# The queries' maxima spread over the partitions: three bfloat16 rows in place of a float32 product with diagonal tiles

## The chip, the cores and the metric

The kernel runs on one core of a Trainium2 chip. The metric is the device time of one execution in microseconds (us). Runs of the same kernel are compared by their median.

## What is computed

The input x has 4 batches of 2048 tokens of 512 features, in float32. Two layers follow each other. The first is causal attention with one head of width 512 and with relu on its projections; the second is a feed-forward layer with two top-32 gates. The change lies in the attention:

```python
q = jax.nn.relu(x @ Wq + bq)
k = jax.nn.relu(x @ Wk + bk)
v = jax.nn.relu(x @ Wv + bv)
e = jnp.einsum('bqd,bkd->bqk', q, k) / jnp.sqrt(jnp.float32(D))
...
e = e - NEG * causal[None, :, :]
e = jnp.exp(e - jnp.max(e, axis=-1, keepdims=True))
attn = e / jnp.sum(e, axis=-1, keepdims=True)
y = jnp.einsum('bqk,bkd->bqd', attn, v)
return jax.nn.relu(y @ Wo + bo)
```

What matters here is the maximum of each query's scores, which is subtracted before the exponential.

## The kernel before

The tokens are worked on in 16 groups of 512 (four groups g = 0 to 3 in each batch), each of four tiles of 128 tokens. Phase 1 (`phase1`) does the attention, the residual sum and the norms; phase 2 (`phase2`) does the feed-forward layer tile by tile. Between them the results go through memory. A second branch of the program, with `every_key=True`, is there for inputs with very large scores; it holds the same functions and is not executed here.

Scores are kept with keys on the partitions: a score tile `n.st[kt]` has 128 keys on the partitions and the group's 512 queries along the free dimension. So the maximum over the keys is a maximum across partitions, and it has to be available on every partition, along the free dimension, to be subtracted. This is how it is made:

- VectorE folds the score tiles into `n.mx` (128 x 512) with elementwise maxima (`masked` L688, `maximum` L589).
- `fold` (L707) turns its four 128x128 blocks on TensorE into PSUM (L711).
- `reduced` (L714) takes the maximum along the free dimension on VectorE (L717). The result is 128 x 4: query q of tile t stands in partition q, column t.
- `diagonals` (L720) multiplies the identity by each of the four columns on VectorE (L725). This gives four 128x128 tiles with the maxima on their diagonals.
- `spread` (L727) multiplies a 128x128 tile of ones with these 512 columns in one float32 product on TensorE (L730). Every partition of `n.mb` in PSUM then holds all 512 maxima.
- `weights` (L732) subtracts `n.mb` from each score tile on VectorE (L738), takes the exponential on ScalarE (L739) and sums up on GpSimd (L743).
- `attend` (L768) multiplies the weights with the values (L773), and `summed` (L748) takes the sums over the keys.

The matrix products are float32, and the profile shows each as two matmul instructions (two passes). Projections and products with keys of earlier groups are done by class `Seven` (L523) with seven block products in place of eight; each of its steps `p1` to `p7` is eight matmul instructions of 256 columns (L555). A step that ends an accumulation is written out by `written` (L592): VectorE adds a partial result (L607) and ScalarE applies bias and relu (L614).

The order of the work is written out by hand in `steps` (L906) for TensorE, VectorE and GpSimd. ScalarE's order is left to the framework's scheduler; some of its instructions have a raised priority (`tc.high_priority()`). TensorE's order is the program's. VectorE's order comes from a small planner, `Pace` (L224): it keeps a modelled time of TensorE (`pace.pe(us)` moves it on) and of VectorE, and it puts queued jobs (`pace.add(rank, job)`) into VectorE's stream where the model says that there is time; `pace.flush(job)` puts a job there at once if it is not there yet. Around the change (L976 to L989) the order is: `fold`; the job `diagonals` is queued at rank 0; then the steps Q.p2, Q.p5, V.p7, Q.p1 and V.p4 of the next group's projections; then `spread` and the queuing of `weights`. In the last group there is no next group: two pieces of a filler, `bound` (L861, matmuls L869, followed by an activation L877 on ScalarE), stand between `fold` and `spread`.

In phase 2, `logits` (L1215) begins with a bfloat16 product of three rows (L1218): `ones3`, a 3 x 128 tile of ones, with a bias that is stored as three bfloat16 rows whose sum is the float32 bias. A product of one column (L1428) stands near the end of phase 2.

Of the kernel before, what the change touches and what calls it, by code (L numbers as in the profile page):

```python
# [28 lines left out]
F32 = mybir.dt.float32  # L29
BF16 = mybir.dt.bfloat16  # L30
I32 = mybir.dt.int32
AF = mybir.ActivationFunctionType
ALU = mybir.AluOpType
# [6 lines left out]
P = 128  # L40
GT = 512
TPG = GT // P
# [11 lines left out]
def sandwich_kernel(ctx: ExitStack, tc: tile.TileContext, io: dict, out: bass.AP):  # L54
    nc = tc.nc
    x = io["L0_attn_x"]
    B, S, D = x.shape
    C2 = io["L0_ffn_weight"].shape[1]
    NG = io["L0_ffn_so_conv_w"].shape[0]
    NC = D // P  # L60
# [10 lines left out]
    const = ctx.enter_context(tc.tile_pool(name="const", bufs=1))  # L71
    dram = ctx.enter_context(tc.tile_pool(name="dram", bufs=1, space=DRAM))

    ident = const.tile([P, P], F32, name="ident")
    make_identity(nc, ident)

    causal = const.tile([P, P], F32, name="causal")
    nc.gpsimd.memset(causal, 0.0)
# [3 lines left out]
    ones = const.tile([P, P], F32, name="ones")  # L82
# [30 lines left out]
    ones3 = const.tile([3, P], BF16, name="ones3")  # L113
# [82 lines left out]
    def phase1(every_key):  # L196
# [8 lines left out]
        sm = enter("sm", 4)  # L205
        two = enter("two", 2)
# [8 lines left out]
        ps_tp = enter("ps_tp", 2, space=PSUM)  # L215
# [4 lines left out]
        def combine(out, a, b, op, factor=1.0):  # L220

            nc.vector.scalar_tensor_tensor(out, a, factor, b, ALU.mult, op)  # L222
# [54 lines left out]
        pace = Pace()  # L277

        def work(us, fn, *args, pause=0.0):

            fn(*args)
            yield us, pause
# [34 lines left out]
        def at_once(pieces):  # L317
            for _ in pieces:
                pass
# [81 lines left out]
        parts = lambda m: [(AS_RIGHT if m == "o" else AS_LEFT)[k] for k in ORDER]  # L401
# [305 lines left out]
        def fold(src):  # L707

            tp = ps_tp.tile([P, NC, P], F32, name="tp")
            for t in range(TPG):  # L710
                nc.tensor.transpose(tp[:, t, :], src[:, t * P : (t + 1) * P], ident)  # L711
            return tp

        def reduced(tp, op):  # L714

            r = sm.tile([P, TPG], F32, name="fold")
            nc.vector.tensor_reduce(r, tp, axis=AX.X, op=op)  # L717
            return r

        def diagonals(n, tp):  # L720

            m = reduced(tp, ALU.max)
            n.dg = two.tile([P, TPG, P], F32, name="xn")
            for t in range(TPG):
                nc.vector.tensor_scalar_mul(n.dg[:, t, :], ident, m[:, t : t + 1])  # L725

        def spread(n):  # L727

            n.mb = ps_mm.tile([P, GT], F32, name="mm")
            nc.tensor.matmul(n.mb, lhsT=ones, rhs=n.dg.rearrange("p t q -> p (t q)"), start=True, stop=True)  # L730

        def weights(n):  # L732

# [127 lines left out]
        def bound():  # L861

            w = ring.take("q", range(NC))
            for d in range(NC):
                ps = ps_mm.tile([P, GT], F32, name="mm")
                for c in range(NC):
                    nc.tensor.matmul(  # L869
                        ps, lhsT=w[c][1][:, d * P : (d + 1) * P], rhs=w[c][1], start=(c == 0), stop=(c == NC - 1)  # L870
                    )
                    if c % 2:
                        pace.pe(1.72)
                    if c == 1:
                        yield
                sqr = prp.tile([P, D], F32, name="pr")
                nc.scalar.activation(sqr, ps, AF.Square, accum_out=squared[:, 0, d : d + 1])  # L877
                yield

        def prepare(br):  # L880

            j = branches.index(br)
            nc.sync.dma_start(gamma2[:, j : j + 1], io[f"L0_ffn_{br}_gamma"].rearrange("(p o) -> p o", o=1))
            nc.sync.dma_start(beta2[:, j : j + 1], io[f"L0_ffn_{br}_beta"].rearrange("(p o) -> p o", o=1))
            lin, left = (stp.tile([P, D], F32, name="st") for _ in range(2))
            nc.sync.dma_start(
                lin.rearrange("p (c g) -> p c g", c=NC), io[f"L0_ffn_{br}_lin_w"].rearrange("(c p) g -> p c g", p=P)
            )
            nc.sync.dma_start(left[0:1, :], io[f"L0_ffn_{br}_lin_b"].rearrange("(o n) -> o n", o=1))
            return lin, left[0:1, :]  # L890

        def bias_rows(br, left):

            wide = prp.tile([P, D], F32, name="pr")[0:1, :]
            for k in range(3):
                row = prep.tile([1, C2], BF16, name="row")
                nc.vector.tensor_copy(row, left)
                nc.sync.dma_start(lin_3[br][k : k + 1, :], row)
                if k < 2:
                    nc.vector.tensor_copy(wide, row)  # L900
                    combine(left, left, wide, ALU.subtract)
                yield 1.5, 2.0
# [3 lines left out]
        def steps(n, ahead):  # L906
# [3 lines left out]
            for j in range(NGRP):  # L910
                nxt = ahead
                last = nxt is None
                filler = bound() if last else None
                if j in (1, 2):
                    lin, left = prepare(branches[j - 1])
# [43 lines left out]
                else:  # L959
                    V = Seven(nxt, "v")  # L960
# [15 lines left out]
                if ahead is not None:  # L976
                    measured = pace.add(1, moments(ahead), 2.0)
                tp = fold(n.mx)
                dg = pace.add(0, work(1.8, diagonals, n, tp))
                pace.pe(0.45)  # L980
                if last:
                    next(filler), next(filler)
                else:
                    Q = Seven(nxt, "q")
                    Q.p2(), Q.p5(), V.p7(), Q.p1(), V.p4()
                pace.flush(dg)
                spread(n)
                pace.pe(0.86)
                weighted = pace.add(1, weights(n))  # L989
                if not last:  # L990
                    if stored:
# [14 lines left out]
                if j in (1, 2):  # L1006
                    br = branches[j - 1]
                    transposed(ps_tp, lin, lin_T[br].rearrange("p (c o) -> p c o", c=NC), nc.scalar.copy)
                    rows = pace.add(1, bias_rows(br, left))
                if last:  # L1010
                    next(filler)

# [23 lines left out]
                            behind.append(pace.add(2, chain(n, u), 2.0))  # L1036
                pace.flush(*evicted)
                if j in (1, 2):
                    pace.flush(rows)
                if last:  # L1040
                    pace.drain()
                    features(n, 0)
# [9 lines left out]
                before, n = n, nxt  # L1052
# [4 lines left out]
        n = load(*order[0], queues=(nc.sync, nc.sync if every_key else nc.scalar))  # L1057
# [15 lines left out]
        if every_key:  # L1073
            bo = broadcast(wp, "L0_attn_bo")
            for b in range(B):
                kTs, vos = [], []
                for g in range(GB):
                    if b + g:
                        n = load(b, g)
                        at_once(moments(n))  # L1080
                    transpose_x(n)
                    drop(project(n, "v"))
                    drop(project(n, "k"))
                    drop(project_vo(n))
                    kTs.append(n.kT)
                    vos.append(n.vo)
                for g in range(GB):
                    n = load(b, g)
                    at_once(moments(n))
                    transpose_x(n)  # L1090
                    drop(project(n, "q"))
                    no_scores(n)
                    for kt in range(n.nk):
                        score_tile(n, kt, kTs[kt // TPG])
                    diagonals(n, fold(n.mx))
                    spread(n)
                    at_once(weights(n))
                    inverses(n, summed(n.sum))
                    n.a, n.xg, n.xr = [None] * TPG, [None] * TPG, [None] * TPG
                    for t in range(TPG):  # L1100
                        load_residual(n, t)
                        attended(n, t, attend(n, t, vos))
                        at_once(chain(n, t))
                        if n.i == NGRP - 1:
                            features(n, t)
                    if n.i < NGRP - 1:
                        fetch_features(n.i)
                        pace.drain()
        else:

            transpose_x(n)
            ahead = load(*order[1])
            at_once(moments(ahead))
            for m in "vqk":
                w = project(n, m)
                weight_sums(m, w)
                if m == "k":
                    squares(w)
                drop(w)
            w = project_vo(n)  # L1120
            ahead.ahead = [normed(ahead, t) for t in range(2)]
            weight_sums("o", w)
            drop(w)
            head.close()

            bo = broadcast(wp, "L0_attn_bo")
            for br in branches:
                nc.gpsimd.dma_start(
                    conv_w[br],
                    io[f"L0_ffn_{br}_conv_w"].rearrange("g f -> (g f)").rearrange("(o n) -> o n", o=1).broadcast_to((P, D)),  # L1130
                )
            with tc.manual_schedule(engines={PE, mybir.EngineType.DVE, mybir.EngineType.Pool}):
                steps(n, ahead)
# [346 lines left out]
```

## Time and profile before

| | |
|---|---|
| median of 3 runs | 2429.8 us (2428.56 to 2430.73) |
| the profiled execution | 2428.93 us |
| its span in the trace | 2427.1 us |
| granted TensorE clock, mean | 0.994 |
| TensorE matmul busy | 2374.7 us (98%) |
| VectorE busy | 1796.1 us (74%) |
| ScalarE busy | 1118.2 us (46%) |
| L730, product with the diagonals | 32 matmul instructions in 16 groups, 592 ns each |
| L725, diagonals | 64 instructions, 281 ns each |
| L717, maximum along the free dimension | 16 instructions, 680 ns each |
| L1218, product of three bfloat16 rows | 128 matmul instructions, 374 to 384 ns each |

The span is the time from the first to the last instruction in the trace; the execution's own time is 1.8 us longer. Lines of the profile name the engine (PE is TensorE, DVE VectorE, ACT ScalarE, POOL GpSimd), the line of the kernel, the operation, the tile written and the tiles read, the shape, and the count. Matmuls overlap: a matmul's duration is longer than the time until the next one starts, so the time that a row of matmuls takes from TensorE is read from the starts. In lines of the timeline the first column is the start in us from the span's start, the second the duration, and what stands in brackets at the end is the idle time of the engine before it and what ended it.

### The profile page before, as it was taken

To read this page: it belongs to the slowest core of one execution; us is meant where nothing else is said; L and a number is where in the kernel's file an instruction comes from. 1 tells how busy PE (TensorE), PEld (TensorE's weight loads), DVE (VectorE), ACT (ScalarE), POOL (GpSimd) and SP (SyncE) were. 2 spreads that over 40 slices of the span, in tenths; PEclk is the share of its full clock that TensorE was granted. 3 is DMA by queue.
4 is the path that set the end of the run, shared out by engine and by line. 5 is a ranking of instruction groups with operands and counts; after the bars stand their busy time and mean duration, and the time that the engine had idled before them with its cause. 6 is when DMAs were issued, how large, how long until landed. Compare 5 with 4: busy or idle time off the path is not lost.

```text
span 2427.1 us, 29394 instructions
## 1 busy us (share of the span) xinstructions
PE 2374.7 (98%) x8418; PEld 1531.5 (63%) x8418; DVE 1796.1 (74%) x3941; ACT 1118.2 (46%) x2352; POOL 900.7 (37%) x856
## 2 busy tenths in 40 slices
PE   8999999999999999999999999999889999999997
PEld 3776858587685858768585776857334444444443
DVE  3587775558866555886655588655599999999998
ACT  2333423233342323334233334322268888888887
POOL 1012211311221031122103112211269999999997
PEclk9999999999999999999999999999999999999999
DMA  6587755568775656876565677633433444444441
GB/s 222 179 244 203 215 166 166 145 178 236 217 204 165 165 144 183 227 220 202 168 166 142 184 224 211 194 117 88 121 74 98 112 122 113 122 113 118 117 122 54
DMA packets 594735, 392.18 MB, mean 162 GB/s; under 512 B 393090, under 2 KB 460162, under 8 KB 594564
## 3 DMA queue, kind: packets, MB, share of 16 engines
q1 hardware_dynamic: 590932, 386.53, 57.6%
q10 hardware_dynamic: 3312, 2.63, 0.4%
q8 instruction: 70, 1.15, 0.2%
q0 software_dynamic: 320, 1.05, 0.1%
q14 instruction: 101, 0.83, 0.1%
HBM read 275.26 MB, written 114.82 MB: 161 GB/s over the span
## 4 chain that ended last, share of the span: by engine, by line
PE 73%; DVE 19%; ACT 3%; issue 3%; POOL 1%; DMA 0%; POOLq 0%; ACTq 0%
PE acc L555 24%; PE acc L773 19%; PE mm L555 17%; PE mm L673 5%; DVE m_si L1227 4%; DVE rest_so L1235 3%; DVE m_so L1227 3%; DVE rest_si L1235 3%; PE mm L1294 2%; PE mm L408 2%; DVE rest_so L1238 2%; DVE rest_si L1238 1%; ACT sq L1268 1%; PE lg L1220 1%; ACT sq L1265 1%
## 5 line engine op out<-in xcount | busy, mean ns | idle before, releaser
L773 PE MATMUL acc<-vo,st 128*128 128x512 f32 x1088 | 475.9, 593 | 0.0
L773 PEld LDWEIGHTS acc<-vo,st 128*128 128x128 f32 x1088 | 205.3, 190 | 239.8 <-issue 234.3
L1294 PE MATMUL mm<-w_L_ffn_weight,xsT 128*128 128x512 f32 x512 | 232.0, 596 | 2.6 <-ACT xsT L165 1.4
L1294 PE MATMUL mm<-w_L_ffn_weight,xnT 128*128 128x512 f32 x512 | 232.1, 596 | 0.0
L137 POOL TENSOR_TENSOR rs_a<-ve_a,neg_half 128x1 f32<-128x1 f32 x64 | 38.4, 600 | 489.7 <-DVE ve_a L146 483.7
L1294 PEld LDWEIGHTS mm<-w_L_ffn_weight,xsT 128*128 128x128 f32 x512 | 98.0, 192 | 127.0 <-issue 113.4
L1294 PEld LDWEIGHTS mm<-w_L_ffn_weight,xnT 128*128 128x128 f32 x512 | 97.7, 191 | 122.1 <-issue 118.2
L555 PE MATMUL mm<-xnT,wb 128*128 128x256 f32 x720 | 170.1, 379 | 0.0
L555 PE MATMUL acc<-T,wb 128*128 128x256 f32 x720 | 170.1, 379 | 0.0
L743 POOL TENSOR_TENSOR mxsum<-mxsum,st 128x512 f32<-128x512 f32 (+2 forms) x144 | 162.5, 1128 | 14.7 <-ACT st L739 4.3
L137 POOL TENSOR_TENSOR rstd_x<-var_x,neg_half 128x4 f32<-128x4 f32 (+1 forms) x19 | 17.8, 936 | 403.1 <-DVE var_x L310 398.8
L555 PE MATMUL acc<-xnT,wb 128*128 128x256 f32 x720 | 165.2, 379 | 0.0
L555 PEld LDWEIGHTS acc<-xnT,wb 128*128 128x128 f32 x720 | 136.8, 190 | 25.0 <-issue 6.5
L555 PEld LDWEIGHTS acc<-T,wb 128*128 128x128 f32 x720 | 136.8, 190 | 25.0 <-issue 6.5
L555 PEld LDWEIGHTS mm<-xnT,wb 128*128 128x128 f32 x720 | 135.3, 190 | 24.0 <-issue 7.2
L673 PE MATMUL mm<-qT,kT 128*128 128x128 f32 (+3 forms) x512 | 148.6, 433 | 0.0
L574 ACT COPY cp<-mm 128x512 f32<-128x512 f32 x72 | 42.2, 586 | 203.6 <-PE mm L555 200.0
L222 DVE SCALAR_TENSOR_TENSOR mxsum<-mxsum,st 128x512 f32<-128x512 f32 (+2 forms) x144 | 86.4, 600 | 65.9 <-ACT st L601 61.3
L1227 DVE MAX8 m_si<-rest_si 128x8 f32<-128x512 f32 x192 | 130.4, 679 | 0.1
L1227 DVE MAX8 m_so<-rest_so 128x8 f32<-128x512 f32 x192 | 128.9, 671 | 0.0
L1235 DVE MATCH_REPLACE8 rest_so<-m_so,rest_so 128x512 f32<-128x512 f32 x192 | 128.8, 671 | 0.0
L1235 DVE MATCH_REPLACE8 rest_si<-m_si,rest_si 128x512 f32<-128x512 f32 x192 | 128.8, 671 | 0.0
(238 smaller groups left out, 4902.1 us busy)
## 6 DMA issues: line engine op xcount, KB each, us to landing
wb<-keys SPq DMA_DIRECT2D x168, 256.0 KB, 2.9
x<-x SPq DMA_DIRECT2D x124, 256.0 KB, 3.0
xr<-in_L_attn_x_dram SPq DMA_DIRECT2D x64, 256.0 KB, 3.8
xn<-xn SPq DMA_DIRECT2D x64, 256.0 KB, 2.8
out_dram<-h SPq DMA_DIRECT2D x64, 256.0 KB, 2.0
xt<-in_L_attn_x_dram SPq DMA_DIRECT2D x62, 256.0 KB, 3.2
wb<-Z_v SPq DMA_DIRECT2D x60, 256.0 KB, 2.8
wb<-Z_q SPq DMA_DIRECT2D x60, 256.0 KB, 3.1
```

The lines of the kernel that those rows point to most:

```text
L137: nc.gpsimd.tensor_tensor(dst, src, neg_half[:, : src.shape[1]], ALU.pow)
L222: nc.vector.scalar_tensor_tensor(out, a, factor, b, ALU.mult, op)
L408: nc.tensor.matmul(ps, lhsT=w[c][1][:, d * P : (d + 1) * P], rhs=xnT[:, c, :], start=(c == 0), stop=(c == NC - 1))
L555: nc.tensor.matmul(ps[:, d * H : (d + 1) * H], lhsT=left[:, c, d * P : (d + 1) * P], rhs=right[:, c, :], start=(new and c + d == 0), stop= ...
L574: nc.scalar.copy(t, ps)
L673: nc.tensor.matmul(ps[:, off:], lhsT=kT[:, c, k : k + P], rhs=n.qT[:, c, off:], start=(c == 0), stop=(c == NC - 1),)
L743: nc.gpsimd.tensor_tensor(n.sum[:, off:], n.sum[:, off:], w, ALU.add)
L773: nc.tensor.matmul(acc, lhsT=n.st[kt][:, t * P : (t + 1) * P], rhs=vos[kt // TPG][:, kt % TPG, :], start=(kt == 0), stop=(kt == nk - 1),)
L1227: nc.vector.max(n.m8[br], n.rest[br] if k else n.lg[br])
L1235: nc.vector.match_replace(n.rest[br], n.m8[br], n.rest[br], -LOWEST)
L1238: nc.vector.match_replace(n.rest[br], n.m8[br], n.lg[br], -LOWEST)
L1294: nc.tensor.matmul(ps, lhsT=lhsT[:, c, :], rhs=wf[:, c, :], start=(c == 0), stop=(c == NC - 1))
```

## The change

The step `diagonals` is replaced by two, `thirds` on VectorE and `rows` on TensorE and ScalarE, and `spread` is made from what these give.

- `thirds` splits the 128 x 4 maxima into three bfloat16 parts whose sum is the float32 value: it copies to bfloat16, copies back to float32, subtracts, and so on. These are seven small VectorE instructions, each of which reads the result of the one before.
- `rows` turns the parts, tile by tile, with a bfloat16 identity: four matmuls, each with three stationary columns and 128 moving columns, give a 3 x 512 tile in PSUM. ScalarE copies it to SBUF as bfloat16.
- `spread` multiplies `ones3` (three rows) with these 512 columns in one bfloat16 product.
- In the order of the work, `rows` goes ahead of V.p4, and `spread` stays behind V.p4. In the last group, `rows` goes between the two filler pieces. The planner's figures change with it: 1.3 in place of 1.8 us for the VectorE job, and 0.25 at `rows` and 0.25 at `spread` in place of 0.86 us of TensorE.
- A bfloat16 identity is made once at the start. A variable is renamed from `rows` to `linear`.

```diff
+    ident16 = const.tile([P, P], BF16, name="ident16")
+    nc.vector.tensor_copy(ident16, ident)
...
-        def diagonals(n, tp):
+        def thirds(n, tp):
 
             m = reduced(tp, ALU.max)
-            n.dg = two.tile([P, TPG, P], F32, name="xn")
+            n.parts = sm.tile([P, 3, TPG], BF16, name="parts")
+            wide = sm.tile([P, TPG], F32, name="wide")
+            for k in range(3):
+                nc.vector.tensor_copy(n.parts[:, k, :], m)
+                if k < 2:
+                    nc.vector.tensor_copy(wide, n.parts[:, k, :])
+                    combine(m, m, wide, ALU.subtract)
+
+        def rows(n):
+
+            tp = ps_tp.tile([P, NC, P], F32, name="tp")
             for t in range(TPG):
-                nc.vector.tensor_scalar_mul(n.dg[:, t, :], ident, m[:, t : t + 1])
+                nc.tensor.matmul(
+                    tp[0:3, t, :],
+                    lhsT=n.parts[:, :, t],
+                    rhs=ident16,
+                    start=(t == 0),
+                    stop=(t == TPG - 1),
+                    skip_group_check=True,
+                )
+            n.rows = two.tile([P, 2 * D], BF16, name="xn")[0:3, :GT]
+            with tc.high_priority():
+                nc.scalar.copy(n.rows, tp[0:3, :, :].rearrange("p t q -> p (t q)"))
+            pace.pe(0.25)
 
         def spread(n):
 
             n.mb = ps_mm.tile([P, GT], F32, name="mm")
-            nc.tensor.matmul(n.mb, lhsT=ones, rhs=n.dg.rearrange("p t q -> p (t q)"), start=True, stop=True)
+            nc.tensor.matmul(n.mb, lhsT=ones3, rhs=n.rows, start=True, stop=True)
...
                 tp = fold(n.mx)
-                dg = pace.add(0, work(1.8, diagonals, n, tp))
+                dg = pace.add(0, work(1.3, thirds, n, tp))
                 pace.pe(0.45)
                 if last:
-                    next(filler), next(filler)
+                    next(filler)
+                    pace.flush(dg)
+                    rows(n)
+                    next(filler)
                 else:
                     Q = Seven(nxt, "q")
-                    Q.p2(), Q.p5(), V.p7(), Q.p1(), V.p4()
-                pace.flush(dg)
+                    Q.p2(), Q.p5(), V.p7(), Q.p1()
+                    pace.flush(dg)
+                    rows(n)
+                    V.p4()
                 spread(n)
-                pace.pe(0.86)
+                pace.pe(0.25)
                 weighted = pace.add(1, weights(n))
...
-                    diagonals(n, fold(n.mx))
+                    thirds(n, fold(n.mx))
+                    rows(n)
                     spread(n)
```

More of the change, by code (lines that the diff above doesn't have):

```diff
@@ L1008, in steps @@
                     transposed(ps_tp, lin, lin_T[br].rearrange("p (c o) -> p c o", c=NC), nc.scalar.copy)
-                    rows = pace.add(1, bias_rows(br, left))
+                    linear = pace.add(1, bias_rows(br, left))
                 if last:
@@ L1038, in steps @@
                 if j in (1, 2):
-                    pace.flush(rows)
+                    pace.flush(linear)
                 if last:
```

## The prediction

> **What bounds the kernel now.** I read the page's busy shares first, then who waited for whom on TensorE in the first phase, then the timeline of TensorE around one group's product L730, then ScalarE and VectorE in the same microseconds, and last the places where the kernel already runs what the change brings in: a bfloat16 product of three rows (L1218) and a stationary tile with very few columns (L1428).
>
> ```profile
> PE 2374.7 (98%) x8418; PEld 1531.5 (63%) x8418; DVE 1796.1 (74%) x3941; ACT 1118.2 (46%) x2352; POOL 900.7 (37%) x856
> ```
>
> That is an average over two phases. The first phase, where the change lies, is read from a window and from TensorE's waits in it:
>
> ```profile
> 20.00:1742.00 1722.00, 1720.66 (x6696) 1244.00 (x6696) 1123.91 (x2286) 564.07 (x1112) 304.52 (x328) 1.00 0.64 181
> ```
>
> ```profile
> PE acc L555 <- DVE vo L607: 1.3, 4, 0.4
> ```
>
> In 1722 us TensorE is idle for 1.3, at full clock; VectorE works 1124, ScalarE 564. So the first phase lasts as long as its stream of matmuls, and the sum for this change is one of TensorE time, plus any wait that it puts into the stream. What it saves on VectorE is worth nothing by itself. The stream around the product that goes, in the first group:
>
> ```profile
> 96.41 1.89 PE L555 MATMUL acc<-T,wb 128*128 128x256 f32 x8
> 98.13 1.02 PE L730 MATMUL mm<-xn,ones 128*128 128x512 f32 x2
> 98.99 1.89 PE L555 MATMUL mm<-xnT,wb 128*128 128x256 f32 x8
> ```
>
> Starts count here, since the ends are modelled and overlap. L730 holds the stream from 98.13 to 98.99: 0.86 us, two passes of 0.43. There is one per group, 16 in all. The block of 96.41 is V.p4, ahead of which the new transposes go.
>
> **What the change removes.** 16 x 0.86 = 13.8 us of TensorE, and on VectorE four multiplications per group (L725, 281 ns each, one begun every 0.2 us, 0.87 together).
>
> **What it adds on TensorE.** Two visits per group from the float32 stream to bfloat16 products that use a part of the array: four 128x128 transposes onto three columns, and one product of three rows with 512 columns. The second exists already, in the second phase:
>
> ```profile
> 1795.12 0.60 PE L164 MATMUL tp<-ident,xs 128*128 128x128 f32 x4
> 1795.65 0.39 PE L1218 MATMUL lg<-lin_si,ones 3*128 3x512 bf16 x1
> 1795.88 0.37 PE L1218 MATMUL lg<-lin_so,ones 3*128 3x512 bf16 x1
> 1796.18 1.12 PE L1220 MATMUL lg<-linT_si,xa_si 128*128 128x512 f32 x2
> 1797.14 1.02 PE L1220 MATMUL lg<-linT_so,xa_so 128*128 128x512 f32 x2
> 1798.00 0.59 PE L1294 MATMUL mm<-w_L_ffn_weight,xsT 128*128 128x512 f32 x1
> ```
>
> By their rates, four transposes take 0.44 (begun every 0.11), two bfloat16 products 0.22 each, four float32 passes 1.72: 2.60 us. From 1795.12 to 1798.00 it is 2.88. The missing 0.28 lies at the borders: 0.09 between the last transpose's end and the first bfloat16 product, 0.08 between the last bfloat16 product's end and float32, and 0.10 in the first float32 pair (0.96 instead of 0.86). It is nearly the same each time that this sequence comes. Whether it is the type or the shape of the tile, this shows:
>
> ```profile
> 2407.75 1.45 PE L1294 MATMUL mm<-w_L_ffn_weight,xnT 128*128 128x512 f32 x3
> 2409.13 0.20 PE L1428 MATMUL mm<-squared,ones 128*1 128x16 f32 x2
> 2409.26 0.66 PE L164 MATMUL tp<-ident,xs 128*128 128x128 f32 x4
> ```
>
> The third pass starts at 2407.75 + 0.86 and ends its turn at 2409.04; L1428, float32 too but on one column, starts 0.09 later. So a narrow tile pays the entry without any change of type, and 128 rows by three columns (the new transposes) should pay like three rows by 128 columns.
>
> Here a rule speaks for the change and another against. By the Trainium skill, TensorE: Matmul & The Clock Gate, section Back-to-back issue gap, a bfloat16 matmul costs its columns at 2.4 GHz plus 2.5 ns: 56 ns for 128 columns, 216 for 512. The rates above agree (0.22). By that rule alone a group costs 4 x 0.056 + 0.216 = 0.44 instead of 0.86, and the change saves 16 x 0.42 = 6.7 us. TensorEngine Tiling (Array Packing), section Key Properties, says that a change of the tiling mode drains the engine. The rows bear the second out, and price it at 0.28 per visit. I take the rows:
>
> - transposes: 0.28 + 4 x 0.056 (estimate from the rate of the rows and that page) = 0.50. No row shows bfloat16 at 128 columns. From below: 0.056 each, and no drain at all if three columns should count as a full tile, 0.22 together. From above: 0.11 each, as the float32 transposes, if each new small stationary tile has to be waited for: 0.72. I take 0.50, because L1218's two loads both run within 0.11 us, ahead of the second product.
> - the product of three rows: 0.28 + 0.22 = 0.50, between narrow bounds, since L1218 is this very shape.
>
> Together 1.00 against 0.86: 0.14 to 0.15 us more per group, 16 groups, +2.4 us. The drain eats the whole saving.
>
> **The other engines.** VectorE: the four multiplications become seven small steps that each need the one before. The nearest rows are chains of that kind (columns: start, duration):
>
> ```profile
> 1757.35 0.16 DVE L1169 TENSOR_TENSOR bnb<-bnb,bna 128x2 f32<-128x2 f32 x1
> 1757.54 0.16 DVE L1170 TENSOR_TENSOR bnb<-bnb,beta 128x2 f32<-128x2 f32 x1
> ```
>
> 0.195 from one to the next, so 7 x 0.195 = 1.35 us in place of 0.87 (1.2 to 1.5, from chains of 0.175 to 0.21 elsewhere). VectorE gets 0.5 us more per group, not less. In groups 0 to 14 the diagonals end 4.5 to 4.9 us before V.p4 starts, so the transposes find their rows ready, with 4 us to spare. Behind the thirds VectorE holds sums for the keys and the next additions; the addition of V.p7 had waited 0.82 us for TensorE, which takes up the 0.5.
>
> ScalarE gets one copy of 512 columns, 0.59 us (L165, L574). TensorE waits for it ahead of the new product, and everything in TensorE's order stands behind that wait. The gap for it, in the first group:
>
> ```profile
> 95.61 0.91 ACT L614 ACTIVATE vT<-vT,bv 128x256 f32<-128x256 f32 x2 [1.86 <-DVE vT L607]
> 97.40 0.91 ACT L614 ACTIVATE qT<-qT,bqk 128x256 f32<-128x256 f32 x2 [0.89 <-DVE qT L607]
> ```
>
> The transposes start at 96.41 + 0.09; the last starts 0.17 later, and a copy follows a last transpose by 0.26 to 0.31 (1795.45 to 1795.76): 96.95 to 97.54. ScalarE is idle from 96.52 to 97.40, so the copy fits and pushes the two qT activations by 0.14; their results are needed blocks later. The product is due at 96.41 + 0.50 + 1.72 = 98.63, 1.1 us after. So the copy costs nothing; without that gap it would cost what it lacks, once per group. The other groups have the same idle stretch to within 0.1 (one 0.4 longer).
>
> The maxima reach VectorE when the product ends: it starts 0.50 later than L730 did, but is over in 0.09 + 0.39 instead of 1.02, so the weights begin about as before. The bfloat16 identity is made once, while VectorE waits for the first x tile until 4.7 us: nothing. PSUM buffers: one more from the pool of two for transposes, whose older user is long read; nothing.
>
> **Where a stall does appear: the last group.** It has no V.p4, only two filler blocks of L869:
>
> ```profile
> 1686.03 3.60 PE L869 MATMUL mm<-wb 128*128 128x512 f32 x8
> 1689.47 1.02 PE L730 MATMUL mm<-xn,ones 128*128 128x512 f32 x2
> ```
>
> ```profile
> 1686.23 0.69 DVE L717 TENSOR_REDUCE fold<-tp 128x4 f32<-128x512 f32 x1 [1.98 <-PE tp L711]
> 1686.96 0.87 DVE L725 TENSOR_SCALAR xn<-ident,fold 128x128 f32<-128x128 f32 x4
> ```
>
> The transposes are due after the first filler block, at 1687.75, and the thirds end at 1686.96 + 1.35 = 1688.3. TensorE waits for about 0.5 us (0.3 to 0.7). The second block then covers ScalarE's copy. The attention that follows has its first weights ready in time: the new product ends at about 1691.1, subtraction and exponential take it to 1692.4, and TensorE is free for it at 1692.8.
>
> **Sum.** +2.4 (drains less savings) + 0.5 (last group) = +2.9. The second phase is untouched and follows the end of the first. The profiled execution of 2428.93 us (span 2427.1, and 1.8 around it) becomes 2431.8; it lies 0.9 below the median of the runs, so 2429.8 + 2.9 = 2432.7. A measurement of this kernel can tell about 0.2%, 4.9 us, from no change: I forecast no change that can be told, a little on the slow side.
>
> **Rivals.**
>
> Slower: the small stationary tiles are not loaded ahead. Place: the four transposes, each with its own three columns. Price: 0.11 each in place of 0.056, 0.22 per group, +3.5 us: 2436.2. For it: L753, eight loads with one-column products, runs at 0.10 each, bound by the load. Against it: those loads have 128 columns, these three. It decides from about 0.087 us per transpose on.
>
> Slower, other place: ScalarE's copy stands behind the two qT activations, which end at 98.31. Then it ends at 98.90 and TensorE waits 0.3 in 15 groups: +4.8, 2437.5. Against it: the copy is raised in priority, and VectorE's addition, for which qT waits, comes out later than the transposes. Akin to it: VectorE's order, which follows from the changed planning costs, lets an addition come late now and then, up to 0.4 us each, as L607's four waits show; a few give 2435.
>
> Faster: no drain, the rates alone. 2429.8 - 6.7 + 0.5 = 2423.6. The rows of L1218 exclude it for the product; for the transposes alone (-0.28 x 16) it gives 2428.2, which is no change.
>
> That the change doesn't do what it says, that is, leaves L730 at 0.86 somewhere, I exclude: both callers go through the new functions.
>
> **Chances.** The forecast's case with its small variants, the undrained transposes among them, 0.68; loads not ahead 0.15; late copy or late additions 0.13; no drain 0.04. The first is no change, the two in the middle are slower: 0.28. The range runs from 2430.0 (half of the drain at the transposes spared) to 2437.0, which takes in the loads and most of the late copy.
>
> **What would show it.** Right: L730 in the new profile starts with 0.09 and 0.08 at its borders and the float32 block behind it loses 0.10; V.p4's first matmul starts 0.4 after Q.p1's turn ends and the product 2.2 after; TensorE's idle time is that of the drains and one wait of 0.5 near 1688. Wrong: transposes 0.1 apart, a wait of the product for ScalarE, a wait of the transposes for VectorE in more groups than the last, or a stream without the gaps.

## The result

The changed kernel takes 2434.49 us (median of 22 runs, 2432.32 to 2436.56) against 2429.98 before (22 runs, 2428.28 to 2432.73): ratio 1.0018, interval 1.0013 to 1.0024. It is slower by 3 to 6 us. The ratio lies within the 0.2% that the forecast called no change (the interval reaches 0.24%), and on the slow side that it named; with 22 runs of each kernel it can be told from no change all the same. The profiled execution has a span of 2430.8 us against 2427.1.

TensorE's timeline in the first group of the changed kernel (starts, durations), where L737 is the four transposes and L753 the product of three rows:

```profile
92.81 3.62 PE L557 MATMUL acc<-xnT,wb 128*128 128x256 f32 x16
96.36 0.39 PE L737 MATMUL tp<-ident,parts 128*3 128x128 bf16 x4
96.68 1.99 PE L557 MATMUL acc<-T,wb 128*128 128x256 f32 x8
98.60 0.38 PE L753 MATMUL mm<-xn,ones 3*128 3x512 bf16 x1
98.92 1.99 PE L557 MATMUL mm<-xnT,wb 128*128 128x256 f32 x8
```

A float32 matmul of 256 columns has its turn for 0.216 us. The sixteen of the first line should end their turn at 92.81 + 3.45 = 96.26; the transposes start 0.10 later. They start 0.056 apart, so their turn ends at 96.58, and V.p4 starts 0.09 to 0.10 later, at 96.68. Its eight matmuls should take 1.73 and L753 should start at 98.41; it starts at 98.60, 0.19 later: 0.10 inside V.p4's first pair, 0.09 at the border. Read from all starts of a group, a visit of the transposes costs 0.515 us and one of the product 0.516, together 1.03 in place of 0.86.

TensorE's waits in the first phase (from 20 to 1745 us) of the changed kernel:

```profile
PE acc L557 <- DVE vo L609: 1.3, 4, 0.4
PE tp L737 <- DVE parts L728: 0.5, 1, 0.5
```

The four waits of before are still there, and one is new. It is in the last group, where L892 is the filler. First TensorE, then VectorE's chain:

```profile
1688.84 1.88 PE L892 MATMUL mm<-wb 128*128 128x512 f32 x4
1691.20 0.39 PE L737 MATMUL tp<-ident,parts 128*3 128x128 bf16 x4 [0.47 <-DVE parts L728]
1691.51 1.98 PE L892 MATMUL mm<-wb 128*128 128x512 f32 x4
```

```profile
1689.76 0.17 DVE L728 CAST parts<-fold 128x4 bf16<-128x4 f32 x1
1689.97 0.17 DVE L730 CAST wide<-parts 128x4 f32<-128x4 bf16 x1
...
1690.97 0.17 DVE L728 CAST parts<-fold 128x4 bf16<-128x4 f32 x1
```

The first filler block's turn ends at 1690.56. The seventh of the small steps, 0.20 apart, ends at 1691.14, and the transposes start 0.06 later. The gap is 0.64, of which 0.10 would have been the border's.

To compare kernels without the start and without the second phase, I take the stretch from the first group's fold to the last attention matmul of phase 1, by their starts in the trace: 1653.23 us before, 1656.89 changed. That is +3.66. It is made up of 16 x 0.172 = 2.75 at the two visits (0.515 + 0.516 - 0.859), 0.54 in the last group and 0.38 at one late addition of VectorE in the second group (below); together 3.67. The runs' +4.5 has an interval of 3.2 to 5.8, in which 3.66 lies; where the rest of the 4.5 lies, if it is real, these two traces don't show.

### The profile page after: what moved, and what is told of

The parts are those of the page before. It is cut to its first block, busy times and chain, and to the rows that moved or that the text cites. A ratio compares the mean times of both kernels' runs of the same rounds, so it can differ in the third digit from the quotient of the medians.

```text
span 2430.8 us, 29518 instructions
## 1 busy us (share of the span) xinstructions
PE 2376.0 (98%) x8466; PEld 1526.4 (63%) x8466; DVE 1796.7 (74%) x3990; ACT 1129.9 (46%) x2368; POOL 900.2 (37%) x856
## 4 chain that ended last, share of the span: by engine, by line
PE 72%; DVE 21%; ACT 3%; issue 2%; POOL 1%; DMA 0%; POOLq 0%; ACTq 0%; DVEq 0%
PE acc L557 24%; PE acc L796 19%; PE mm L557 17%; DVE m_si L1256 5%; PE mm L675 5%; DVE m_so L1256 4%; DVE rest_so L1264 4%; DVE rest_si L1264 3%; PE mm L410 2%; PE mm L1323 2%; DVE rest_so L1267 2%; DVE rest_si L1267 1%; ACT sq L1297 1%; ACT sq L1294 1%; PE lg L1249 1%
## 5 line engine op out<-in xcount | busy, mean ns | idle before, releaser
L766 POOL TENSOR_TENSOR mxsum<-mxsum,st 128x512 f32<-128x512 f32 (+2 forms) x144 | 162.1, 1126 | 18.0 <-ACT st L762 7.4
```

Source lines behind the costliest of these rows:

```text
L766: nc.gpsimd.tensor_tensor(n.sum[:, off:], n.sum[:, off:], w, ALU.add)
```

## The experiments

Theory: TensorE stops at the borders (the two places where the stream goes over to another shape of stationary tile and back) because that tile is narrow in rows or columns, and that eats the saving. Rivals: the change of type between float32 and bfloat16 stops it; or the time comes through VectorE's changed order.

**Both products on the whole array.** The parts are written into 128 columns per tile, and the product reads 128 rows; what is not a part is zero. Sixteen memsets are added on VectorE, and ScalarE copies 128 rows in place of three.

```diff
+            n.wide = two.tile([P, 2 * D], BF16, name="xn")
+            n.parts = n.wide[:, GT:].rearrange("p (t q) -> p t q", t=TPG)
+            nc.vector.memset(n.wide[:, GT:], 0.0)
...
-                    tp[0:3, t, :],
-                    lhsT=n.parts[:, :, t],
+                    tp[:, t, :],
+                    lhsT=n.parts[:, t, :],
...
-            nc.tensor.matmul(n.mb, lhsT=ones3, rhs=n.rows, start=True, stop=True)
+            nc.tensor.matmul(n.mb, lhsT=ones16, rhs=n.rows, start=True, stop=True)
```

> Both products use the whole array: the four transposes have 128 stationary columns (three parts, the rest zeros, set by one memset per group on VectorE ahead of the reduction), and the spreading product has 128 rows of bfloat16 ones. The arithmetic's result is the same, and the types are those of the changed kernel. Theory (the narrow tile's shape is what drains TensorE, 0.29 us per visit): the borders vanish, a group costs 4 x 0.056 + 0.216 = 0.44 us instead of 1.03 (changed) or 0.86 (before); 16 x 0.42 = 6.7 less than before, less the wait of 0.5 in the last group: 6.2 us below before, 2423.8. Rival (the change of type between float32 and bfloat16 is what costs): the borders stay at 0.09 to 0.10 each and the time stays at that of the changed kernel, 2434.5. Second rival (the time went into VectorE's changed order): also 2434.5, with no gaps at the borders to be seen.

Measured: 2426.76 (21 runs) against 2430.0 for the kernel before on the same chip, ratio 0.9987, interval 0.998 to 0.9993. TensorE in the second group of this kernel (L741 the transposes, L757 the product):

```profile
174.78 1.89 PE L559 MATMUL acc<-xnT,wb 128*128 128x256 f32 x8
176.51 0.39 PE L741 MATMUL tp<-ident,xn 128*128 128x128 bf16 x4
176.73 1.95 PE L559 MATMUL acc<-T,wb 128*128 128x256 f32 x8
178.51 0.38 PE L757 MATMUL mm<-xn,ones 128*128 128x512 bf16 x1
178.73 1.89 PE L559 MATMUL mm<-xnT,wb 128*128 128x256 f32 x8
```

174.78 + 1.73 is 176.51: no gap on entering bfloat16. 176.51 + 0.22 is 176.73: none on leaving. The product, 178.51 to 178.73, is as clean. The types are those of the changed kernel, so the type does not stop TensorE; the shape does.

The loads of the stationary tiles (PEld in the profile) show what the stop is. First those of the changed kernel's transposes, then those of this kernel's:

```profile
96.36 0.20 PEld L737 LDWEIGHTS <-parts 128*3 128x3 bf16 x4 [0.33 <-issue]
```

```profile
176.29 0.43 PEld L741 LDWEIGHTS <-xn 128*128 128x128 bf16 x4
```

In this kernel the first load begins 0.21 ahead of its matmul (176.51), while the last float32 matmul still has its turn, as loads do inside the float32 stream. In the changed kernel it begins together with its matmul (96.36). In all 16 groups there, at both visits, the first narrow tile and the first float32 tile behind it are loaded only within 0.005 of their own matmul. So no tile is loaded ahead across a change of shape. The 0.10 that the pair behind loses belongs to it: the second float32 load begins 0.108 after the first, so it comes late too. Why they are not, the traces don't show.

What I had not expected is 0.055 that is still lost in the first pair behind the whole transposes (178.51 - 176.73 is 1.78 instead of 1.73), and not behind the product. The loads explain it: the first float32 load begins 0.054 ahead of its matmul, since the transpose before it has a turn of 0.056 only, and the second load begins 0.110 after the first. Behind a product of 0.216 both come in time. So a group costs 0.22 + 0.055 + 0.216 = 0.495. The stretch fell from 1653.23 (before) to 1648.95: 4.3 us, where 16 x 0.364 = 5.8 come from the products; the last group's wait (0.67) and the late addition (0.83 here, 0.38 in the changed kernel) take back 1.5. The mechanism is as the theory had it, and the gain smaller than the 6.2 that I expected.

**Only one of the two.** The same edits, for the transposes alone (128 columns) and for the product alone (128 rows).

> Only the transposes use the whole array (128 stationary columns, mostly zeros); the spreading product keeps its three rows. Theory (shape): one visit of two stops draining, 16 x 0.29 = 4.6 us below the changed kernel, 2429.9, level with before. Rival (type): no difference from the changed kernel, 2434.5. If loading 128 columns four times can't be hidden, the transposes are about 0.1 us apart instead of 0.056 and 2 to 3 us of the gain are lost.

> Only the spreading product uses the whole array (128 rows, of which 125 are zeros, set by a memset per group); the transposes keep their three columns. Theory (shape): 16 x 0.29 = 4.6 us below the changed kernel, 2429.9. Rival (type): 2434.5.

Measured: 2431.74 (13 runs; ratio to before 1.0005, interval 0.9997 to 1.0013) and 2430.22 (13 runs; 1.0003, 0.9994 to 1.0011). Both are level with before, as expected, and the stretches, 1653.42 and 1652.60, are 3.5 and 4.3 below the changed kernel's, where 4.6 was expected of each. The transposes' part falls short by the 0.055 above, 0.9 in 16 groups; the late additions of VectorE and the last group's wait, both a little longer here, take the rest. The two gains add up to 7.8, and both together gave 7.9. The kernel with whole transposes in the second group:

```profile
176.73 0.39 PE L739 MATMUL tp<-ident,xn 128*128 128x128 bf16 x4
176.96 1.95 PE L557 MATMUL acc<-T,wb 128*128 128x256 f32 x8
178.84 0.38 PE L755 MATMUL mm<-xn,ones 3*128 3x512 bf16 x1
179.15 1.56 PE L557 MATMUL mm<-xnT,wb 128*128 128x256 f32 x6
```

The border at the transposes is gone (0.22 to V.p4) and that at the three-row product is as in the changed kernel (0.31 to the next). Each visit pays for itself, in rows as in columns.

**Three more visits, by shape and type.** Added to the changed kernel, with unused results:

```diff
+            if kind == 0:
+                nc.tensor.matmul(tp[0:3, 0, :], lhsT=ident[:, 0:3], rhs=ident, start=True, stop=True)
+            elif kind == 1:
+                nc.tensor.matmul(tp[0:3, 0, :], lhsT=ident16[:, 0:3], rhs=ident16, start=True, stop=True)
+            else:
+                nc.tensor.matmul(tp[:, 0, :], lhsT=ident16, rhs=ident16, start=True, stop=True)
...
-                    Q.p3(), Q.p6(), K.p2(), K.p5(), Q.p7(), K.p1(), Q.p4(), K.p3(), K.p6()
+                    Q.p3(), Q.p6(), K.p2(), probe(0), K.p5(), Q.p7(), probe(1), K.p1(), Q.p4(), probe(2), K.p3(), K.p6()
```

> The changed kernel with three more visits per group, whose results are not used: one float32 product with three stationary columns behind K.p2, one bfloat16 product with three stationary columns behind Q.p7, one bfloat16 product on the whole array behind Q.p4, each with 128 moving columns. Theory (shape drains): float32 narrow 0.29 + 2 x 0.11 = 0.51, bfloat16 narrow 0.29 + 0.06 = 0.35, bfloat16 full 0.06; together 0.92 per group, 13.8 us in 15 groups (the last has no such steps). Rival (type drains): float32 narrow 0.22, bfloat16 narrow 0.35, bfloat16 full 0.35; together also 0.92, so the trace's borders tell them apart, not the time.

Measured: 2448.91 (4 runs) against 2430.65, ratio 1.0076, interval 1.006 to 1.0091. The stretch is 14.1 us longer than the changed kernel's. The first group:

```profile
104.88 0.38 PE L754 MATMUL tp<-ident 128*3 128x128 f32 x2
105.19 1.99 PE L557 MATMUL mm<-T,wb 128*128 128x256 f32 x8
...
108.85 0.22 PE L756 MATMUL tp<-ident 128*3 128x128 bf16 x1
108.99 1.99 PE L557 MATMUL acc<-xnT,wb 128*128 128x256 f32 x8
...
112.55 0.22 PE L758 MATMUL tp<-ident 128*128 128x128 bf16 x1
112.61 1.73 PE L557 MATMUL mm<-xnT,wb 128*128 128x256 f32 x7
```

From its start to the next block: the float32 one with three columns 0.31 (two passes of 0.11, and 0.09), the bfloat16 one with three columns 0.15 (0.056 and 0.09), the bfloat16 one with 128 columns 0.06, its plain rate. With the 0.09 to 0.10 ahead of the narrow ones and what the next pair loses (0.10, 0.10, 0.056), the three cost 0.51, 0.35 and 0.11 (0.06 had been expected of the last). In 15 groups that is 14.5; the late addition of 0.38 doesn't come here, which leaves the 14.1. Float32 with a narrow tile pays all of the border without any change of type; bfloat16 with a whole tile pays none of it but the half of a weight load that a turn of 0.056 can't hide. The type as the cause is refuted by both.

**The transposes right before the product.** In 15 groups `V.p4()` and `rows(n)` change places:

```diff
-                    rows(n)
                     V.p4()
+                    rows(n)
```

> The changed kernel with the transposes behind V.p4 instead of ahead of it, right before the spreading product, in 15 groups. My account (V.p4 hides ScalarE's copy): TensorE waits for the copy, 0.3 from the last transpose to its start and 0.58 of copying, less the drain that lies in it: 0.8 us per group, +12 us, about 2446; more if V.p4's own activations stand ahead of the copy on ScalarE (0.9 us more per group, +25). Rival (the copy is not what the product waits for): no change.

Measured: 2445.53 (4 runs), ratio to before 1.0063, interval 1.0048 to 1.0079. TensorE's waits in that kernel's first phase, and ScalarE in its first group:

```profile
PE mm L753 <- ACT xn L747: 12.0, 15, 1.0
```

```profile
98.54 0.47 ACT L616 ACTIVATE vT<-acc,bv 128x256 f32<-128x256 f32 x1
98.92 0.56 ACT L747 CAST xn<-tp 3x512 bf16<-3x512 f32 x1
```

The product waits 0.8 us for the copy in the mean, as worked out; in the group shown one of V.p4's activations stands ahead of the copy, not both. The 12 us of waits lengthen the stretch by 9.9 only, since the borders then lie inside the wait. So the place ahead of V.p4 is what keeps ScalarE's copy off the path.

**Five steps instead of seven.** The subtraction reads the bfloat16 part directly:

```diff
-                    nc.vector.tensor_copy(wide, n.parts[:, k, :])
-                    combine(m, m, wide, ALU.subtract)
+                    combine(m, m, n.parts[:, k, :], ALU.subtract)
```

> The changed kernel with five steps instead of seven for the thirds. My account: only the last group's wait shrinks, from 0.5 to 0.1: 0.4 us, 2434.1, no difference that the timing can tell. Rival (VectorE's longer chain delays each group): 6 us less, 2428.

> As the kernel with both products on the whole array, and the thirds made in five steps instead of seven: the subtraction reads the bfloat16 part directly. Theory (VectorE's chain counts in the last group alone, where TensorE waits 0.5 us for it): 2 x 0.2 = 0.4 us less than with seven steps, 2423.4, which the timing alone can hardly tell, and the wait in the last group shrinks from 0.5 to 0.1. Rival (the chain delays VectorE in every group and TensorE behind it): 16 x 0.4 = 6.4 us less.

Measured: on the changed kernel 2434.06 (16 runs; ratio to before 1.0015, interval 1.0007 to 1.0022), which is no difference from 1.0018. Its stretch is 0.36 shorter, all of it in the last group (57.01 us from its fold to the end instead of 57.41). VectorE's longer chain costs nothing in the other groups. On the kernel with whole tiles: 2425.27 (19 runs), ratio 0.998, interval 0.9973 to 0.9987. That is the lowest median of all, 4.7 us below before. In its last group 0.27 is left of the wait of 0.67 (I had expected 0.1): 0.40 less, which is what two steps take. Yet its stretch, 1648.87, is only 0.1 below the one with seven steps, because two other additions of VectorE come late in it (0.28 at 633.6 us, 0.10 at 1106.7). The rest of the 1.5 between the two medians is not seen in the stretch and is not explained by the steps.

## Why the prediction was right, step by step

- **TensorE alone bounds the first phase**: right. The saving on VectorE is nil, as is the cost of its longer chain outside the last group.
- **The border, 0.28 per visit, whatever the type**: right; 0.29 to 0.30 measured. It was read from L1218, where type and shape change together, and from L1428, where the shape changes alone; the three added visits show that L1428 was the row to go by. One figure left a border out: the product was to start 2.2 after Q.p1's turn and starts 2.34 after it, 0.10 of which is the product's own entry.
- **Transposes 0.50 and product 0.50**: 0.515 and 0.516. The transposes are 0.056 apart, the figure of the formula in the Trainium skill (TensorE: Matmul & The Clock Gate, section Back-to-back issue gap). The prediction took that formula for a stream; the page gives it for a lone matmul, and for a stream of loads and matmuls 81 ns at 128 columns and 131 ns at 512. The measured 0.056, four in a row, and 0.216 agree with the formula. The rival with 0.11 each is out. 0.172 more per group instead of 0.14 to 0.15, and 2.75 us instead of 2.4.
- **The copy fits into ScalarE's gap**: right. ScalarE in the first group of the changed kernel:

```profile
95.84 0.91 ACT L616 ACTIVATE vT<-vT,bv 128x256 f32<-128x256 f32 x2 [2.24 <-DVE vT L609]
96.78 0.57 ACT L747 CAST xn<-tp 3x512 bf16<-3x512 f32 x1
97.27 0.90 ACT L616 ACTIVATE qT<-qT,bqk 128x256 f32<-128x256 f32 x2
```

  It ends at 97.35, 1.25 ahead of the product's start (98.60), and the product waits for it in no group. The rival of the late copy is out; its price was 0.3 in 15 groups, which is 4.5 and not 4.8.
- **A wait of 0.5 in the last group**: 0.54. The chain is 7 x 0.20 instead of 7 x 0.195.
- **Late additions**, a minor rival, did come once: in the second group a step starts 0.28 late behind VectorE's addition and its first pair loses 0.10 more, 0.38 in all (0.83 in the kernel with whole tiles). The prediction had such additions among its rivals, at up to 0.4 each, and not in its sum. Ahead of that addition one VectorE instruction (L839, L816 before) takes 1.07 where it took 0.54. In all eight kernels that came after, it begins while an addition of GpSimd (L766 in the changed kernel) is under way, and it ends 0.28 to 0.29 after that one ends, however long it takes (1.07 to 1.51). In the kernel before it begins 0.04 ahead of the end of GpSimd's addition and takes 0.54. So it is GpSimd that it seems to wait for; that is read from these times, and no run was made for it.
- **The rule that speaks for the change** (the rates alone, -6.7 us) fails because the shape's border is not in it; **the rule against it**, TensorEngine Tiling (Array Packing), section Key Properties, that a change of tiling mode drains the engine, is what decided, at the price that this case's rows gave it. The page has no price, and that a narrow tile is a change of mode in its sense is an inference from the stops. With whole tiles the rates alone come near: 0.495 per group instead of 0.44.
- **The sum, +2.9**: 3.66 in the traces. Of the difference 0.35 is the two visits, 0.04 the wait in the last group and 0.38 the late addition.
- **A reading that was off**: the one-column matmuls of L753 are 0.11 apart and not 0.10. Nothing in the sum rests on it.

## What to carry to other kernels

A small product costs its columns and its borders. Before float32 products are split into narrow bfloat16 ones, look in the trace for a place where a tile of few rows or columns already stands in a stream of whole ones, and add up starts there: here 0.3 us per visit, more than a 512-column bfloat16 product. Padding the tile with zeros to the whole array kept the bfloat16 rate and took most of the border away at the transposes and all of it at the product, and turned a slightly slower kernel into a slightly faster one. Only one, three and 128 rows or columns stand in these traces; how wide a tile has to be is open.

## What had not been expected

The last stretch of the time varies for a reason that has nothing to do with the change: at the seam of the phases TensorE's clock is granted by half for several microseconds, in pieces of 3.4 us or multiples of it. Between 1735 and 1800 us that is 14 us in the profile of the kernel before and 20 us in that of the kernel with whole tiles. From the last attention matmul to the end of the span the four kernels before, changed, whole tiles, and whole tiles with five steps took 684.9, 685.0, 688.7 and 684.7 us, although this part is the same in all. The runs of one kernel scatter in the same way: of the 55 runs of the kernel before that were taken beside the whole-tile kernels, the 23 with a mean granted clock of 0.994 took 2428.95 us in the mean, and the 19 with 0.992 took 2430.86. A difference of a few microseconds between the spans of two single profiles is thus no sign of anything; the stretch inside phase 1 and the medians of many runs say more.
